# Sign product of a graph layer with two rows of x in one F32R matmul, interleaved with the first two row blocks of the aggregation

## The chip, the cores and the metric

The kernel runs on one NeuronCore of one Trainium2 chip. The metric is the device time of one execution in microseconds (us). The execution that the profiler recorded spans 2025.5 us. In what follows TensorE is called PE (its weight loads PEld), VectorE DVE, ScalarE ACT, GpSimd POOL and SyncE SP, as in the profile. SBUF is the on-chip memory that all engines read, PSUM the memory that TensorE adds its products into; the kernel uses it as eight banks of 128 x 512 fp32 numbers.

## What is computed

Two graph layers on x (4096 x 512) with an adjacency matrix adj (4096 x 4096), all fp32. The change is in layer 0 alone:

```python
bw = sign(weight)                 # 512 x 512, entries -1, 0, 1
ba = maximum(sign(x), 0.0)        # 4096 x 512, entries 0, 1
xw = ba @ bw.T                    # whole numbers from -512 to 512
x  = layernorm(x + relu(adj @ xw))
# layer 1: x @ edge_w, scores x' @ x'.T, two softmaxes, a product with adj,
# x @ weight and a second layernorm; it takes the larger part of the time
```

The product `ba @ bw.T` is called the sign product below, and `adj @ xw` the aggregation.

## The kernel before

P is 128, W 512 and D 512; NG = 8 groups of 512 rows, BG = 4 row blocks of 128 in each, NB = 32 row blocks in all, KD = 4 slices of 128 columns; HB = 16 and QC = 8. A tile pool hands out buffers: all tiles with one tag share `bufs` buffers, and a tile is written only when an earlier one of its tag has been read for the last time. The synchronisation between engines, and the order of instructions in the queue of each engine, are made by the framework from the data that the instructions touch; the order in the queues can differ from the written one.

The pools that matter: `stream` has 3 buffers (of 8 KB per partition), `rows` 4, `signs` (`sp`, tags `hi` and `lo`) 2 of each tag, `ps_mm` 6 banks of PSUM, `ps_tr` 2.

The sign product. For each group of 512 rows, the transposed x is loaded (`xt`), DVE compares it with zero into a bf16 tile `ba`, PE multiplies four row blocks by four slices, and ACT copies each finished bank into `xw`. In the first group, the weights are prepared slice by slice at the same time; twelve products of zeros run ahead while the first data are on their way.

```python
    warm = wp.tile([P, W], BF16, name="warm")
    nc.vector.memset(warm, 0.0)
    w0 = stream.tile([P, KD, D], F32, name="w0", tag="stream")
    bw = wp.tile([P, KD, D], BF16, name="bw")

    for g in range(NG):
        xt = stream.tile([P, KD, W], F32, name="xt", tag="stream")
        ba = sp.tile([P, KD, W], BF16, name="ba", tag="hi")
        pws = [ps_mm.tile([P, D], F32, name="pw", tag="mm") for j in range(BG)]
        if g == 0:
            neg = sp.tile([P, KD, D], BF16, name="neg", tag="lo")
            for k in range(KD):
                nc.sync.dma_start(w0[:, k, :], w0_t[ts(k, P), :])
                nc.scalar.dma_start(xt[:, k, :], x_t[ts(k, P), ts(g, W)])
            for _ in range(WARM):
                nc.tensor.matmul(pws[0], warm[:, :P], warm, start=True, stop=True)
            for k in range(KD):
                nc.vector.tensor_scalar(neg[:, k, :], w0[:, k, :], 0.0, None, ALU.is_lt)
                nc.vector.tensor_scalar(ba[:, k, :], xt[:, k, :], 0.0, None, ALU.is_gt)
                nc.vector.scalar_tensor_tensor(bw[:, k, :], w0[:, k, :], 0.0, neg[:, k, :], ALU.is_gt, ALU.subtract)
            order = [(k, j) for k in range(KD) for j in range(BG)]
        else:
            nc.sync.dma_start(xt, x_t[:, ts(g, W)].rearrange("(k p) n -> p k n", p=P))
            nc.vector.tensor_scalar(ba, xt, 0.0, None, ALU.is_gt)
            order = [(k, j) for j in range(BG) for k in range(KD)]
        for k, j in order:
            nc.tensor.matmul(pws[j], ba[:, k, ts(j, P)], bw[:, k, :], start=(k == 0), stop=(k == KD - 1))
            if k == KD - 1:
                nc.scalar.copy(xw[:, g * BG + j, :], pws[j])
```

The aggregation of one row block: adj comes in two halves of 16 x 128 x 128, each of which is worked in two quarters. F32R is a 32-bit format that the kernel takes to keep fewer bits than fp32, so ACT rounds a quarter to F32R (`hi`), DVE takes the rest (`lo`), and PE multiplies both with `xw` into one bank: 64 products for a row block. Then follow relu, the sum with x and the normalisation.

```python
    def aggregate(b):
        xb = rows.tile([P, D], F32, name="xb", tag="rows")
        nc.sync.dma_start(xb, x[ts(b, P), :])
        acc = ps_mm.tile([P, D], F32, name="acc", tag="mm")
        for half in range(2):
            at = stream.tile([P, HB, P], F32, name="at", tag="stream")
            nc.sync.dma_start(at, adj_t[b, :, ts(half, HB), :])

            for q in range(2):
                aq = at[:, ts(q, QC), :]
                hi = sp.tile([P, QC, P], F32R, name="hi", tag="hi")
                nc.scalar.copy(hi, aq)
                lo = sp.tile([P, QC, P], F32R, name="lo", tag="lo")
                nc.vector.tensor_sub(lo, aq, hi.bitcast(F32))
                for c in range(QC):
                    kb = half * HB + q * QC + c
                    nc.tensor.matmul(acc, hi[:, c, :], xw[:, kb, :], start=(kb == 0), stop=False)
                    nc.tensor.matmul(acc, lo[:, c, :], xw[:, kb, :], start=False, stop=(kb == NB - 1))
        nc.vector.scalar_tensor_tensor(xb, acc, 0.0, xb, ALU.max, ALU.add)
        layernorm([xb])
        scr = wp.tile([P, D], F32, name="scr")
        nc.vector.tensor_tensor_reduce(
            scr, xb, nw_b, 1.0, 0.0, ALU.mult, ALU.add, accum_out=node_s[:, b : b + 1]
        )
        nc.gpsimd.tensor_add(scr, xb, bias_b)
        nc.gpsimd.dma_start(x1_d[ts(b, P), :], scr)
        return xb
```

The loop over the row blocks takes them in the order 0, 16, 1, 17 and so on. After every second block POOL forms the sums for a later stage (`left`), and PE transposes each block's result with one block's delay:

```python
    before = None
    for n in range(NB):
        b = n // 2 + n % 2 * HB
        xb = aggregate(b)
        if n == 1:
            nc.sync.dma_start(we_s, edge_w.rearrange("(k p) o -> p k o", p=P))
        if n % 2:
            left(n // 2, before[1], xb)
        if before is not None:
            transpose_rows(*before)
        before = (b, xb)
    transpose_rows(*before)
# ... (layer 1 follows)
```

Of the kernel before, what the change touches and what calls it, by code (L numbers as in the profile page):

```python
# [11 lines left out]
F32 = mybir.dt.float32  # L12
BF16 = mybir.dt.bfloat16
F32R = mybir.dt.float32r
AF = mybir.ActivationFunctionType
ALU = mybir.AluOpType
# [3 lines left out]
EPS = 1e-5  # L20
NEG_BIG = -9000000000000000.0
HUGE = 3.4e38
WARM = 12


@with_exitstack
def kernel(
# [34 lines left out]
    make_identity(nc, ident)  # L62
    eps = const.tile([P, 1], F32, name="eps")
    nc.vector.memset(eps, EPS)
    node_s = const.tile([P, NB], F32, name="node_s")

    x1_d = dram.tile([N, D], F32, name="x1_d")
# [79 lines left out]
    with (  # L147
        tc.tile_pool(name="wide", bufs=1) as wide,
        tc.tile_pool(name="stream", bufs=3) as stream,
        tc.tile_pool(name="weights", bufs=1) as wp,  # L150
        tc.tile_pool(name="signs", bufs=2) as sp,
    ):
        x1T = wide.tile([P, KD, N], F32, name="x1T")

        warm = wp.tile([P, W], BF16, name="warm")
        nc.vector.memset(warm, 0.0)
        w0 = stream.tile([P, KD, D], F32, name="w0", tag="stream")
        bw = wp.tile([P, KD, D], BF16, name="bw")

        for g in range(NG):  # L160
            xt = stream.tile([P, KD, W], F32, name="xt", tag="stream")
            ba = sp.tile([P, KD, W], BF16, name="ba", tag="hi")
            pws = [ps_mm.tile([P, D], F32, name="pw", tag="mm") for j in range(BG)]
            if g == 0:
                neg = sp.tile([P, KD, D], BF16, name="neg", tag="lo")
                for k in range(KD):
                    nc.sync.dma_start(w0[:, k, :], w0_t[ts(k, P), :])
                    nc.scalar.dma_start(xt[:, k, :], x_t[ts(k, P), ts(g, W)])
                for _ in range(WARM):
                    nc.tensor.matmul(pws[0], warm[:, :P], warm, start=True, stop=True)  # L170
                for k in range(KD):
                    nc.vector.tensor_scalar(neg[:, k, :], w0[:, k, :], 0.0, None, ALU.is_lt)
                    nc.vector.tensor_scalar(ba[:, k, :], xt[:, k, :], 0.0, None, ALU.is_gt)
                    nc.vector.scalar_tensor_tensor(bw[:, k, :], w0[:, k, :], 0.0, neg[:, k, :], ALU.is_gt, ALU.subtract)
                order = [(k, j) for k in range(KD) for j in range(BG)]
            else:
                nc.sync.dma_start(xt, x_t[:, ts(g, W)].rearrange("(k p) n -> p k n", p=P))
                nc.vector.tensor_scalar(ba, xt, 0.0, None, ALU.is_gt)
                order = [(k, j) for j in range(BG) for k in range(KD)]
            for k, j in order:  # L180
                nc.tensor.matmul(pws[j], ba[:, k, ts(j, P)], bw[:, k, :], start=(k == 0), stop=(k == KD - 1))  # L181
                if k == KD - 1:
                    nc.scalar.copy(xw[:, g * BG + j, :], pws[j])

        nw_b = wp.tile([P, D], F32, name="nw_b")
        nc.sync.dma_start(nw_b, bass.AP(tensor=node_w.tensor, offset=node_w.offset, ap=[[0, P], [1, D]]))
        bias_b = wp.tile([P, D], F32, name="bias_b")
        nc.sync.dma_start(bias_b, bass.AP(tensor=bias.tensor, offset=bias.offset, ap=[[0, P], [1, D]]))
        we_s = wp.tile([P, KD, D], F32, name="we_s")


        def aggregate(b):
            xb = rows.tile([P, D], F32, name="xb", tag="rows")
            nc.sync.dma_start(xb, x[ts(b, P), :])
            acc = ps_mm.tile([P, D], F32, name="acc", tag="mm")
            for half in range(2):
                at = stream.tile([P, HB, P], F32, name="at", tag="stream")
                nc.sync.dma_start(at, adj_t[b, :, ts(half, HB), :])

# [20 lines that stand above are left out]
        def left(b, low, high):  # L220

            to = lop_d[b // BG][:, :, b % BG, :]
            l11, l21, l12, l22 = low[:, :HD], low[:, HD:], high[:, :HD], high[:, HD:]
            sums_l = wp.tile([P, 4, HD], F32, name="sums_l", bufs=2)
            s4, s1, s2, s3 = (sums_l[:, n, :] for n in range(4))
            nc.gpsimd.tensor_sub(s3, l11, l21)
            nc.gpsimd.tensor_add(s1, l22, l21)
            nc.gpsimd.tensor_sub(s2, s1, l11)
            nc.gpsimd.tensor_sub(s4, l12, s2)
            nc.gpsimd.dma_start(to[:, 0, :], l11)  # L230
            nc.gpsimd.dma_start(to[:, 1:4:2, :], high.rearrange("p (h f) -> p h f", h=2))
            nc.gpsimd.dma_start(to[:, 2, :], s4)
            nc.gpsimd.dma_start(to[:, 4:, :], sums_l[:, 1:, :])

        def transpose_rows(b, xb):
            pt = ps_tr.tile([P, KD, P], F32, name="pt", tag="tr")
            for k in range(KD):
                nc.tensor.transpose(pt[:, k, :], xb[:, ts(k, P)], ident)  # L238
            nc.scalar.copy(x1T[:, :, ts(b, P)], pt)
# [15 lines that stand above are left out]
        hT = big.tile([P, KD, N], F32, name="hT", tag="large")  # L255
        HK = KD // 2

        lops = stream.tile([P, 4, HK, HD], F32, name="lops", tag="stream")
        l11, l12 = we_s[:, :HK, :HD], we_s[:, HK:, :HD]
        l21, l22 = we_s[:, :HK, HD:], we_s[:, HK:, HD:]  # L260
        s4, s1, s2, s3 = (lops[:, n] for n in range(4))
        nc.gpsimd.tensor_add(s1, l21, l22)
        nc.gpsimd.tensor_sub(s2, s1, l11)
        nc.gpsimd.tensor_sub(s3, l11, l21)
        nc.gpsimd.tensor_sub(s4, l12, s2)
        left_h = l11, l12, s4, l22, s1, s2, s3
        for g in range(HG):
            r11, r12 = (x1T[:, :HK, ts(c, W)] for c in (g, g + HG))
            r21, r22 = (x1T[:, HK:, ts(c, W)] for c in (g, g + HG))
            t1, t2 = (sp.tile([P, HK, W], F32, name="t12", tag="hi") for _ in range(2))  # L270
            t3, t4 = (sp.tile([P, HK, W], F32, name="t34", tag="lo") for _ in range(2))
            nc.vector.tensor_sub(t1, r12, r11)
            nc.gpsimd.tensor_sub(t3, r22, r12)
            nc.vector.tensor_sub(t2, r22, t1)
            nc.vector.tensor_sub(t4, r21, t2)
            right_h = r11, r21, r22, t4, t1, t2, t3
            seven(
                lambda m, q: [left_h[m][:, k, ts(q, P)] for k in range(HK)],
                lambda m: [right_h[m][:, k, :] for k in range(HK)],
                [[hT[:, q + f, ts(c, W)] for f in (0, HK) for c in (g, g + HG)] for q in range(2)],  # L280
                lambda *_: None,
            )
# [357 lines left out]
```

## Time and profile before

| what | value |
|---|---|
| time, median of 3 runs | 2028.5 us (2028.37 to 2031.58) |
| span of the profiled execution | 2025.5 us, 17,689 instructions |
| PE / DVE / ACT / POOL busy | 99% / 61% / 34% / 20% |
| granted PE clock | 0.998 of full speed |
| moved by DMA | 455.73 MB, mean 225 GB/s |
| sign product on PE | 128 matmuls, starts from 6.2 to 37.3 us |
| aggregation of row blocks 0 and 16 on PE | 128 matmuls, starts from 37.3 to 66.6 us |

How to read it: a group of instructions is shown as line of the kernel, engine, operation, what it writes and reads, shape and count; after the first bar the busy time in us and the mean duration of one in ns; after the second the time the engine stood idle just ahead of them and what released it. Matmuls overlap, so the duration of one is its latency, and the rate is read from the distance between starts in the timeline. The profile names an idle time after the event that ended it; idle time of an engine that is not the limit costs nothing.

### The profile page before, as it was taken

The numbers are of one execution on the slowest core, as the hardware profiler recorded it, in microseconds if no ns is written. First come the engines' busy times: TensorE is split into PE (matmuls) and PEld (weight loads), VectorE is DVE, ScalarE is ACT, GpSimd is POOL, SyncE is SP. The second block draws the span as 40 slices with busy tenths as digits, with TensorE's granted clock in tenths as the row PEclk, the third lists the DMA queues.
The fourth block names the chain that finished last, engine by engine and source line by source line (L and its number), as shares of the span: only waits on it lengthen the run. The fifth ranks groups of instructions, "written<-read, shape, count | busy, mean of one in ns | idle before, by whom it ended". The sixth has DMA issues, their size and how long they took to land.

```text
span 2025.5 us, 17689 instructions
## 1 busy us (share of the span) xinstructions
PE 2004.4 (99%) x6268; PEld 1108.3 (55%) x6268; DVE 1243.5 (61%) x1759; ACT 691.5 (34%) x1195; POOL 401.5 (20%) x485
## 2 busy tenths in 40 slices
PE   9999999999999999999999999999999999999997
PEld 4888888888544454545555444444444444444443
DVE  3555555556534554445545897786759775977634
ACT  4333333333113666666666521131221220222100
POOL 0243333334300000000001111140124111321101
PEclk9999999999999999999999999999999999999999
DMA  9566566565009786867767887765666765685421
GB/s 328 186 220 203 196 216 210 201 209 173 29 0 351 260 302 229 308 231 272 280 257 265 330 329 258 250 248 198 249 237 251 260 246 201 227 283 201 172 70 62
DMA packets 118153, 455.73 MB, mean 225 GB/s; under 512 B 10288, under 2 KB 10288, under 8 KB 93488
## 3 DMA queue, kind: packets, MB, share of 16 engines
q0 software_dynamic: 48128, 241.20, 31.6%
q1 hardware_dynamic: 69360, 212.36, 31.6%
q8 instruction: 49, 0.80, 0.2%
q10 hardware_dynamic: 576, 1.05, 0.1%
q14 instruction: 40, 0.33, 0.0%
HBM read 355.99 MB, written 98.57 MB: 224 GB/s over the span
## 4 chain that ended last, share of the span: by engine, by line
PE 96%; DMA 3%; DVE 1%; ACT 0%; issue 0%; SPq 0%; ACTq 0%; POOLq 0%; POOL 0%; DVEq 0%
PE ps L479 38%; PE pe L356 21%; PE acc L209 11%; PE acc L208 11%; PE po L531 5%; PE seven L89 5%; PE pt L377 3%; DMA a<-in_adj_dram 2%; PE pw L181 1%; PE pt L238 1%; DMA xt<-in_x_t_dram 1%; DVE lo L205 0%; PE ptm L405 0%; DMA xb<-x_d 0%; ACT a L342 0%
## 5 line engine op out<-in xcount | busy, mean ns | idle before, releaser
L356 PE MATMUL pe<-hT 128*128 128x512 f32 (+3 forms) x1152 | 475.5, 557 | 0.0
L479 PE MATMUL ps<-q,lop 128*128 128x512 f32 x1024 | 446.9, 592 | 0.0
L208 PE MATMUL acc<-xw,hi 128*128 128x512 f32 x1024 | 401.6, 392 | 0.0
L209 PE MATMUL acc<-xw,lo 128*128 128x512 f32 x1024 | 399.4, 390 | 0.6 <-DVE lo L205 0.5
L479 PE MATMUL ps<-t,lop 128*128 128x512 f32 x768 | 332.9, 592 | 0.0
L479 PEld LDWEIGHTS ps<-q,lop 128*128 128x128 f32 x1024 | 193.9, 190 | 240.8 <-issue 237.0
L356 PEld LDWEIGHTS pe<-hT 128*128 128x128 f32 x1152 | 205.0, 191 | 184.0 <-issue 174.8
L434 ACT ACTIVATE q<-q 128x2048 f32<-128x2048 f32 x64 | 122.3, 1911 | 407.8 <-DVE q L431 394.2
L205 DVE TENSOR_TENSOR lo<-at,hi 128x1024 fp32r<-128x1024 f32 x128 | 168.7, 1318 | 147.1 <-ACT hi L203 147.1
L479 PEld LDWEIGHTS ps<-t,lop 128*128 128x128 f32 x768 | 145.9, 190 | 183.7 <-issue 180.3
L440 DVE SCALAR_TENSOR_TENSOR q<-ac,q 128x512 f32<-128x512 f32 x256 | 198.9, 830 | 53.6 <-ACT q L434 39.1
L203 ACT CAST hi<-at 128x1024 fp32r<-128x1024 f32 x128 | 134.6, 1052 | 272.6 <-PE acc L208 271.3
L209 PEld LDWEIGHTS acc<-xw,lo 128*128 128x128 f32 x1024 | 192.3, 188 | 41.0 <-DVE lo L205 1.7
L208 PEld LDWEIGHTS acc<-xw,hi 128*128 128x128 f32 x1024 | 192.3, 188 | 39.3
L338 DVE CUSTOM_DVE_ANT_0 a<-a,pe 128x512 f32<-128x512 f32 x112 | 76.7, 687 | 206.9 <-ACT s L363 206.9
L342 ACT ACTIVATE a<-a,nmax_c 128x512 f32<-128x512 f32 x256 | 183.5, 718 | 45.8 <-DVE nmax_c L338 45.5
L483 DVE TENSOR_TENSOR over<-over,ps 128x512 f32<-128x512 f32 x168 | 113.6, 681 | 107.8 <-PE ps L479 107.7
L431 DVE CUSTOM_DVE_ANT_1 q<-q,mrow 128x2048 f32<-128x2048 f32 x64 | 148.5, 2325 | 40.3 <-DMA q<-s_d 36.2
L363 ACT COPY s<-pe 128x512 f32<-128x512 f32 (+2 forms) x144 | 77.7, 543 | 138.4 <-PE pe L356 120.3
L531 PE MATMUL po<-over 128*128 128x512 f32 x256 | 115.9, 600 | 3.7 <-DVE xb L540 3.7
L425 POOL DMA_DIRECT2D ac<-in_adj_t_dram x64 | 48.8, 763 | 325.3 <-DVE q L440 253.4
L377 PEld LDWEIGHTS pt<-ident,s 128*128 128x128 f32 x496 | 62.1, 141 | 68.7 <-issue 57.7
(107 smaller groups left out, 1553.8 us busy)
## 6 DMA issues: line engine op xcount, KB each, us to landing
at<-in_adj_t_dram SPq DMA_DIRECT2D x64, 1024.0 KB, 5.1
ac<-in_adj_t_dram POOLq DMA_DIRECT2D x64, 1024.0 KB, 6.7
a<-in_adj_dram SPq DMA_DIRECT2D x64, 1024.0 KB, 7.5
q<-s_d POOLq DMA_DIRECT2D x64, 1024.0 KB, 7.8
lop<-lop_d SPq DMA_DIRECT2D x112, 512.0 KB, 4.1
s_d<-s POOLq DMA_DIRECT2D x36, 1024.0 KB, 4.8
s_d<-t POOLq DMA_DIRECT2D x28, 1024.0 KB, 6.2
xb<-in_x_dram SPq DMA_DIRECT2D x32, 256.0 KB, 3.1
```

Source lines behind the costliest of these rows:

```text
L203: nc.scalar.copy(hi, aq)
L205: nc.vector.tensor_sub(lo, aq, hi.bitcast(F32))
L208: nc.tensor.matmul(acc, hi[:, c, :], xw[:, kb, :], start=(kb == 0), stop=False)
L209: nc.tensor.matmul(acc, lo[:, c, :], xw[:, kb, :], start=False, stop=(kb == NB - 1))
L342: lambda: nc.scalar.activation(e, e, AF.Exp, bias=nmax_c[:, b, c : c + 1], scale=-1.0, accum_out=sum_c[:, b, c : c + 1])
L356: nc.tensor.matmul(pe[:, lo * P :], hT[:, k, ts(A * BG + i, P)], hT[:, k, (B * BG + lo) * P : (B + 1) * W], start=(k == 0), stop=(k == KD ...
L377: nc.tensor.transpose(pt[:, j, :], s[:, i, ts(j, P)], ident)
L431: nc.vector._custom_dve(TENSOR_ADD_SAT, out=q, in0=q, in1=mrow.unsqueeze(1).to_broadcast([P, BG, W]), s0=0.0, s1=-HUGE)
L434: nc.scalar.activation(q, q, AF.Exp)
L440: nc.vector.scalar_tensor_tensor(qc, a[:, :, c, :], 0.0, qc, ALU.max, ALU.mult)
L479: nc.tensor.matmul(ps, lop[:, c, ts(h, P)], rop[m][:, c, :], start=(c == 0), stop=(c == BG - 1))
L531: nc.tensor.matmul(po, (lower if k // 2 else upper)[:, k % 2, ts(i, P)], w1_s[:, k, :], start=(k == 0), stop=(k == KD - 1),)
```

## The change

It has two parts.

The first part computes two rows of x in one product. For rows a and b of the same group (b lies 256 rows further), `ba` now holds [a > 0] + 2048 [b > 0], in F32R. A product with the signs of the weights gives p = A + 2048 B in fp32, where A and B are the two wanted whole numbers, at most 512 in size, so both can be had from p exactly. Adding SHIFT = 1.5 x 2^34 rounds to a multiple of 2048, so u = SHIFT + 2048 B' (ACT); u - SHIFT - p is then minus the low part (DVE, out of PSUM), and a scaled copy of u gives minus the high part (ACT). The signs of the weights are negated (`bw` is now [w < 0] - [w > 0]), so the minus goes away. The number of sign products falls from 128 to 64, each with 128 x 128 weights and 512 columns as before, in F32R instead of bf16.

The second part moves the aggregation of row blocks 0 and 16 into the loop over the groups. As soon as a group's 512 rows of `xw` exist, the part of adj that meets them (4 x 128 x 128 for each of the two blocks) is loaded, split into hi and lo, and multiplied: 16 products for each group, written one group behind the sign product. Their two sums stay in the two `ps_tr` banks until the end; `aggregate` then finds them ready for these two blocks and does only the rest of its work. The purpose is to use the stretch of the sign product, in which the transfers of x are at work, for multiplications as well.

The buffers: the compare with the factor 2048 (`over0`) takes the tag `hi`, the incoming adj parts and the shifted sums `u` share the four `rows` buffers, `ba` shares a new tag `quarter` (2 buffers) with the later `sums_l`, and `bw` shares the buffer of `we_s`.

The diff, from the definitions on:

```diff
@@ -20,6 +20,8 @@
 EPS = 1e-5
 NEG_BIG = -9000000000000000.0
 HUGE = 3.4e38
+TWO = 2.0**11
+SHIFT = 1.5 * 2.0**34
 WARM = 12
 
 
@@ -62,6 +64,9 @@
     make_identity(nc, ident)
     eps = const.tile([P, 1], F32, name="eps")
     nc.vector.memset(eps, EPS)
+    shift = const.tile([P, 2], F32, name="shift")
+    nc.vector.memset(shift[:, 0:1], SHIFT)
+    nc.vector.memset(shift[:, 1:2], SHIFT / TWO)
     node_s = const.tile([P, NB], F32, name="node_s")
 
     x1_d = dram.tile([N, D], F32, name="x1_d")
@@ -155,32 +160,84 @@
         warm = wp.tile([P, W], BF16, name="warm")
         nc.vector.memset(warm, 0.0)
         w0 = stream.tile([P, KD, D], F32, name="w0", tag="stream")
-        bw = wp.tile([P, KD, D], BF16, name="bw")
-
-        for g in range(NG):
+
+
+        bw = wp.tile([P, KD, D], F32R, name="bw", tag="we_s")
+        assert D * 2 < TWO
+
+        def whole(g):
+
             xt = stream.tile([P, KD, W], F32, name="xt", tag="stream")
-            ba = sp.tile([P, KD, W], BF16, name="ba", tag="hi")
-            pws = [ps_mm.tile([P, D], F32, name="pw", tag="mm") for j in range(BG)]
+            ba = wp.tile([P, KD, W // 2], F32R, name="ba", tag="quarter", bufs=2)
+            pws = [ps_mm.tile([P, D], F32, name="pw", tag="mm") for j in range(BG // 2)]
+            order = [(k, j) for j in range(BG // 2) for k in range(KD)]
+
+            def signs(k, over):
+                a, b = xt[:, k, : W // 2], xt[:, k, W // 2 :]
+                nc.vector.tensor_scalar(over, b, 0.0, TWO, ALU.is_gt, ALU.mult)
+                nc.vector.scalar_tensor_tensor(ba[:, k, :], a, 0.0, over, ALU.is_gt, ALU.add)
+
             if g == 0:
-                neg = sp.tile([P, KD, D], BF16, name="neg", tag="lo")
+
+                pos = sp.tile([P, KD, D], BF16, name="pos", tag="lo")
+                over = sp.tile([P, KD, W // 2], F32, name="over0", tag="hi")
                 for k in range(KD):
                     nc.sync.dma_start(w0[:, k, :], w0_t[ts(k, P), :])
                     nc.scalar.dma_start(xt[:, k, :], x_t[ts(k, P), ts(g, W)])
                 for _ in range(WARM):
                     nc.tensor.matmul(pws[0], warm[:, :P], warm, start=True, stop=True)
                 for k in range(KD):
-                    nc.vector.tensor_scalar(neg[:, k, :], w0[:, k, :], 0.0, None, ALU.is_lt)
-                    nc.vector.tensor_scalar(ba[:, k, :], xt[:, k, :], 0.0, None, ALU.is_gt)
-                    nc.vector.scalar_tensor_tensor(bw[:, k, :], w0[:, k, :], 0.0, neg[:, k, :], ALU.is_gt, ALU.subtract)
-                order = [(k, j) for k in range(KD) for j in range(BG)]
+                    nc.vector.tensor_scalar(pos[:, k, :], w0[:, k, :], 0.0, None, ALU.is_gt)
+                    signs(k, over[:, k, :])
+                    nc.vector.scalar_tensor_tensor(bw[:, k, :], w0[:, k, :], 0.0, pos[:, k, :], ALU.is_lt, ALU.subtract)
+                order = [(k, j) for k in range(KD) for j in range(BG // 2)]
             else:
                 nc.sync.dma_start(xt, x_t[:, ts(g, W)].rearrange("(k p) n -> p k n", p=P))
-                nc.vector.tensor_scalar(ba, xt, 0.0, None, ALU.is_gt)
-                order = [(k, j) for j in range(BG) for k in range(KD)]
+                over = sp.tile([P, KD, W // 2], F32, name="over0", tag="hi")
+                nc.vector.tensor_scalar(over, xt[:, :, W // 2 :], 0.0, TWO, ALU.is_gt, ALU.mult)
+                nc.vector.scalar_tensor_tensor(ba, xt[:, :, : W // 2], 0.0, over, ALU.is_gt, ALU.add)
             for k, j in order:
                 nc.tensor.matmul(pws[j], ba[:, k, ts(j, P)], bw[:, k, :], start=(k == 0), stop=(k == KD - 1))
                 if k == KD - 1:
-                    nc.scalar.copy(xw[:, g * BG + j, :], pws[j])
+
+                    u = rows.tile([P, D], F32, name="u", tag="rows")
+                    nc.scalar.activation(u, pws[j], AF.Identity, bias=shift[:, 0:1])
+                    b = g * BG + j
+                    nc.vector.scalar_tensor_tensor(xw[:, b, :], u, SHIFT, pws[j], ALU.subtract, ALU.subtract)
+                    nc.scalar.activation(xw[:, b + BG // 2, :], u, AF.Identity, bias=shift[:, 1:2], scale=-1.0 / TWO)
+
+
+        early = [0, HB]
+        accs = []
+
+        def halves(g):
+
+            hi = sp.tile([P, QC, P], F32R, name="hi", tag="hi")
+            lo = sp.tile([P, QC, P], F32R, name="lo", tag="lo")
+            for n, b in enumerate(early):
+                a = rows.tile([P, BG, P], F32, name="a0", tag="rows")
+                nc.sync.dma_start(a, adj_t[b, :, ts(g, BG), :])
+                nc.scalar.copy(hi[:, ts(n, BG), :], a)
+                nc.vector.tensor_sub(lo[:, ts(n, BG), :], a, hi[:, ts(n, BG), :].bitcast(F32))
+            return hi, lo
+
+        def follow(g, hi, lo):
+            if g == 0:
+                accs.extend(ps_tr.tile([P, D], F32, name="acc0", tag="tr") for _ in early)
+            for n in range(2):
+                for c in range(BG):
+                    kb = g * BG + c
+                    nc.tensor.matmul(accs[n], hi[:, n * BG + c, :], xw[:, kb, :], start=(kb == 0), stop=False)
+                    nc.tensor.matmul(accs[n], lo[:, n * BG + c, :], xw[:, kb, :], start=False, stop=(kb == NB - 1))
+
+        whole(0)
+        parts = halves(0)
+        for g in range(NG):
+            if g + 1 < NG:
+                whole(g + 1)
+            follow(g, *parts)
+            if g + 1 < NG:
+                parts = halves(g + 1)
 
         nw_b = wp.tile([P, D], F32, name="nw_b")
         nc.sync.dma_start(nw_b, bass.AP(tensor=node_w.tensor, offset=node_w.offset, ap=[[0, P], [1, D]]))
@@ -192,8 +249,8 @@
         def aggregate(b):
             xb = rows.tile([P, D], F32, name="xb", tag="rows")
             nc.sync.dma_start(xb, x[ts(b, P), :])
-            acc = ps_mm.tile([P, D], F32, name="acc", tag="mm")
-            for half in range(2):
+            acc = accs[early.index(b)] if b in early else ps_mm.tile([P, D], F32, name="acc", tag="mm")
+            for half in range(0 if b in early else 2):
                 at = stream.tile([P, HB, P], F32, name="at", tag="stream")
                 nc.sync.dma_start(at, adj_t[b, :, ts(half, HB), :])
 
@@ -221,7 +278,7 @@
 
             to = lop_d[b // BG][:, :, b % BG, :]
             l11, l21, l12, l22 = low[:, :HD], low[:, HD:], high[:, :HD], high[:, HD:]
-            sums_l = wp.tile([P, 4, HD], F32, name="sums_l", bufs=2)
+            sums_l = wp.tile([P, 4, HD], F32, name="sums_l", tag="quarter", bufs=2)
             s4, s1, s2, s3 = (sums_l[:, n, :] for n in range(4))
             nc.gpsimd.tensor_sub(s3, l11, l21)
             nc.gpsimd.tensor_add(s1, l22, l21)

```

## The prediction

> **What bounds the kernel now.** I read the page first: busy time by engine, then the chain of work that ended last, then the groups of instructions.
>
> ```profile
> PE 2004.4 (99%) x6268; PEld 1108.3 (55%) x6268; DVE 1243.5 (61%) x1759; ACT 691.5 (34%) x1195; POOL 401.5 (20%) x485
> PE 96%; DMA 3%; DVE 1%; ACT 0%; issue 0%; SPq 0%; ACTq 0%; POOLq 0%; POOL 0%; DVEq 0%
> ```
>
> TensorE is busy for 99% of the span and 96% of the ending chain is TensorE. So a microsecond of matmul taken out comes off the end, unless a wait takes its place, and the change touches only the first 67 us. I therefore asked for busy time by stretch (columns: stretch and its length; busy us and instructions of PE, PEld, DVE, ACT, POOL; TensorE clock; DMA share; GB/s).
>
> ```profile
> 6.20:16.70 10.50, 7.73 (x33) 2.92 (x31) 6.32 (x11) 3.94 (x8) 0.00 (x0) 1.00 1.04 379
> 16.70:37.50 20.80, 20.73 (x97) 9.51 (x97) 6.97 (x7) 14.55 (x25) 0.00 (x0) 1.00 1.03 398
> 37.50:67.00 29.50, 29.44 (x131) 24.03 (x130) 13.38 (x16) 10.77 (x13) 4.02 (x4) 1.00 0.62 211
> ```
>
> The first two stretches are the sign product, the third is the first two row blocks of the aggregation. In the sign product the transfers are at their limit (about 390 GB/s, DMA share 1) and TensorE is full from 16.7 us on; before that it lost 2.8 us. In the aggregation TensorE is full, VectorE is at 45% (13.38 of 29.5), ScalarE at 37% and the transfers at 62%. The two stages have complementary slack: that is what the change goes for.
>
> The groups of instructions in the first 80 us give the prices:
>
> ```profile
> L208 PE MATMUL acc<-xw,hi 128*128 128x512 f32 x91 | 35.7, 393 | 0.0
> L181 PE MATMUL pw<-bw,ba 128*128 128x512 bf16 x128 | 28.6, 379 | 2.8 <-DVE ba L178 1.6 <-DVE bw L174 1.3
> L183 ACT CAST xw<-pw 128x512 fp32r<-128x512 f32 x32 | 18.3, 588 | 15.2 <-PE pw L181 15.1
> L205 DVE TENSOR_TENSOR lo<-at,hi 128x1024 fp32r<-128x1024 f32 x12 | 17.1, 1421 | 17.8 <-ACT hi L203 17.7
> L203 ACT CAST hi<-at 128x1024 fp32r<-128x1024 f32 x13 | 13.7, 1052 | 24.9 <-PE acc L208 23.7 <-PE acc L209 1.3
> L178 DVE TENSOR_SCALAR ba<-xt 128x2048 bf16<-128x2048 f32 x7 | 8.6, 1227 | 12.9 <-DMA xt<-in_x_t_dram 6.7 <-PE pw L181 6.2
> ```
>
> The mean of a matmul (379, 393 ns) is its latency. What counts is the distance of starts, which the timeline of TensorE shows:
>
> ```profile
> 16.77 20.89 PE L181 MATMUL pw<-bw,ba 128*128 128x512 bf16 x96 [0.24 <-DVE ba L178]
> ...
> 38.29 0.40 PE L208 MATMUL acc<-xw,hi 128*128 128x512 f32 x1
> ...
> 66.63 0.39 PE L209 MATMUL acc<-xw,lo 128*128 128x512 f32 x1
> ```
>
> Sign products (bf16): (20.89 - 0.38) / 95 = 216 ns apart. Aggregation (F32R): the 126 starts from 38.29 to 66.63 lie 227 ns apart (the trace lists 38.29, 38.52, 38.75 and so on; a transpose sits just behind the last). So F32R costs 5% more than bf16 per product of this shape, not a multiple.
>
> **What the Trainium skill says.** (1) "TensorE: Matmul & The Clock Gate", section "Wait — 56ns, not 53.3ns?", gives 215.7 ns between back-to-back warm matmuls of 512 columns; the trace has 216 for bf16. (2) The same page, "Weight-path perf modes — Fast Weight Load (FWL) and DoubleRow", says that the fast weight load is not for FP32. The trace agrees: a weight load takes 98 ns for the bf16 signs and 188 ns for the F32R aggregation. Both are shorter than the matmul beside which they lie, so the longer load should not show; 227 against 216 ns is all that I charge. (3) "VectorE: DVE Perf Modes", "Mode 2×_2P — use both read ports for one tensor", says that an fp32 operation with one tensor input can give two results a cycle from SBUF and one with two inputs cannot. The trace has 1227 ns for 2048 elements of the compare (one input) and 1.22 us for 1024 elements of the split's subtraction (two inputs). (4) "Perfetto Trace Analysis", "Identifying the Most-Contended Engine" warns that repeating gaps can mean that tiles cannot be allocated; this bears on the second rival.
>
> **The change, part by part.**
>
> *TensorE, signs.* Two rows share one product, so 16 matmuls per group become 8: 128 x 0.216 = 27.6 us become 64 x 0.227 = 14.5 us. That takes 13.1 us out, all of it on the path.
>
> *TensorE, aggregation.* The two row blocks keep their 128 matmuls, 128 x 0.227 = 29.0 us, in eight parts of 16 (3.63 us). Only their place changes.
>
> *VectorE, for each group of 512 rows.* Compare of 1024 elements with a factor: about 0.69 us (estimate from the 1227 ns row: fixed 0.16, then half of the rest). Compare-and-add of 1024 elements with two inputs: 1.23 (as the subtraction in L205 where nothing disturbs it). Two subtractions that take the low part out of PSUM: 2 x 0.69 (as the 692 ns of the 128x512 scalar_tensor_tensor in L210). Two lo halves of 512 elements: 2 x 0.69. Sum 4.7 us.
>
> *ScalarE, for each group.* Two shifted copies, two for the high part, two hi halves, six times some 0.58 us: 3.5 us.
>
> *Transfers.* 1.05 MB of x and 0.52 MB of adj for each group, 1.57 MB / 390 GB/s = 4.0 us.
>
> *TensorE, for each group.* 8 x 0.227 + 3.63 = 5.4 us. This is the largest of the four, so TensorE stays the bound if the engines run ahead of each other. VectorE at 4.7 is close behind.
>
> *The start.* The first group's VectorE work grows by about 0.23 us for each of four slices (half-width compare and add instead of one compare), so its last weights come at some 11.4 instead of 10.5 us and its eight products end near 12.1. The second group's x landed at 11.6 us before; 0.69 + 1.23 us of VectorE work bring its products to about 13.6. From there TensorE has 7 x 1.81 + 29.0 = 41.7 us of work. With no wait this ends at **55.3 us**, against 66.9 before: 11.6 us is the most that there can be. The two blocks' normalisation then comes at once, under the third block's matmuls, on a VectorE at 45%, and should cost nothing.
>
> *What I take off.* The shared VectorE queue is in order, and the new steps hand over from PE to ACT to DVE to ACT several times in each group. I allow half a microsecond in each of seven groups, 3.5 us. Gain 11.6 - 3.5 = 8.1 us: 2028.5 - 8.1 = **2020.4 us**, rounded to 2020.5.
>
> **The rivals.** (A) *The order of the queues.* If VectorE kept strictly to the written order, the compare for group g+2 would stand behind the lo halves of group g+1, which stand behind ScalarE's four PSUM steps of that group, which wait for its products. One turn would then be: products 1.8, landing 0.2, shift copy 0.58, high part 0.58, two hi copies 1.16, last lo 0.69, compare and add 1.92, hand-overs 0.5: 7.4 us instead of 5.4. Seven turns more than eat the gain: 7 x 2.0 = 14 us on top of 55.3, about 70 to 78 us for the stage, and 2032 to 2040 in all. Against it speaks that the trace before shows engines out of the written order: in block 0 a lo split runs between the two halves of the normalisation, and hi of the first block runs before the last three xw copies. I give this 8%.
>
> (B) *Buffers.* `rows` has four buffers, now shared by the shifted sums u and the incoming a; `hi` has two, shared by the compare's output and hi. In each group hi stays occupied from its copy to the end of its part, at least 0.58 x 2 + 0.69 + 3.63 = 5.5 us, so two buffers are just enough beside the compare's 1.9 us (7.4 us of 2 x 5.4). And an a can be fetched only when a u or an a came free; xb in the trace took 3.3 us to land at the median and up to 8.2. A late landing stalls hi, then lo, then TensorE. This would cost one or two us in some groups, up to 8 us in all, which leaves a time near the one before. I give it one in four in a strong form; the mild form is in the 3.5 us.
>
> (C) *The transfers.* 2.1 + 7.3 + 4.2 MB = 13.6 MB at 390 GB/s from about 1.7 us on are through at 36.6 us, long before the last group is needed at some 48 us. So bandwidth as such is not the bound. The early groups, though, are fed at 4.0 us each from 11.6 us on and want 5.4, so only the start can be short, by a microsecond or two.
>
> **Range and chances.** The best is 2028.5 - 11.6 = 2017; one more for the scatter between runs gives 2016 as the low end. A VectorE that is held in a few turns, or buffers in a strong form, leave 2025 to 2029; 2029 is the high end. Rival A alone lies outside. Two per cent are 40 us, more than the whole stage can win, and more than even rival A loses, so "within 2%" gets 0.985, faster 0.005, slower 0.01.
>
> **What would show it.** In the profile after: 64 sign matmuls and 128 of the two blocks, with starts 227 ns apart; TensorE done with both blocks at 57 to 61 us; VectorE's busy share in that stretch at 70% or more. Rival A would show as TensorE idle before the sign product, released by the compare-and-add on VectorE, about 2 us in each group; rival B as hi or a waiting for TensorE's last read or for a transfer. If the gaps sit between 6 and 16 us, my start was wrong; if the stretch from 67 us on has changed in length, something beyond the two blocks moved. Wrong would be the F32R price if sign matmuls lie more than 240 ns apart.

## The result, and the profile after

The changed kernel takes **2045.71 us** (median of 4 runs, 2043.21 to 2048.88) against 2028.72 us for the kernel before, a ratio of 1.0081 [1.0064, 1.0099]: 17 us slower, where the prediction had 8 us faster and a range up to 2029.

The page after, first line of the busy times and the chain that ended last:

```profile
PE 2006.6 (98%) x6204; PEld 1113.8 (54%) x6204; DVE 1256.9 (61%) x1796; ACT 696.6 (34%) x1203; POOL 403.1 (20%) x485
PE 94%; DMA 3%; DVE 1%; issue 0%; ACT 0%; SPq 0%; POOLq 0%; POOL 0%; ACTq 0%; DVEq 0%
```

TensorE lost its 64 matmuls (6268 to 6204), yet its busy time is no smaller and its share of the chain fell by two points. The last transpose of the aggregation starts at 542.7 us in the profiled run, against 523.0 before: 19.7 of the 21.6 us by which the two profiled spans differ are there (the profiled run is the slowest of the four), so nearly everything lies ahead of it. Busy time by stretch of the changed kernel (columns as in the prediction):

```profile
6.20:16.70 10.50, 3.83 (x9) 1.44 (x8) 6.62 (x16) 2.48 (x4) 0.00 (x0) 0.69 1.01 336
16.70:37.50 20.80, 13.55 (x48) 9.85 (x48) 8.97 (x12) 8.27 (x13) 0.00 (x0) 0.83 0.65 218
37.50:67.00 29.50, 23.34 (x77) 16.98 (x78) 15.79 (x21) 12.45 (x20) 0.00 (x0) 0.85 0.47 161
67.00:96.50 29.50, 26.61 (x104) 20.21 (x104) 16.45 (x25) 14.37 (x20) 7.43 (x8) 0.92 0.69 232
```

After 16.7 us nothing is full any more. Up to 67 us TensorE issues 125 matmuls where the kernel before issued 228; VectorE is busy for about half the time; the transfers are down from 398 and 211 to 218 and 161 GB/s; the granted clock is 0.83 and 0.85. Every engine and the transfers have slack at once, so the time goes into waits. The groups of the first 100 us name what TensorE waits for:

```profile
L230 PE MATMUL acc<-xw,hi 128*128 128x512 f32 x64 | 29.2, 457 | 19.1 <-ACT hi L220 19.1
L200 PE MATMUL pw<-bw,ba 128*128 128x512 f32 x64 | 19.6, 446 | 2.2 <-DVE ba L178 2.2
L220 ACT CAST hi<-a 128x512 fp32r<-128x512 f32 x16 | 9.6, 617 | 14.0 <-DMA a<-in_adj_t_dram 12.6 <-DVE over L197 1.3
L206 DVE SCALAR_TENSOR_TENSOR xw<-u,pw 128x512 fp32r<-128x512 f32 x16 | 10.9, 688 | 21.9 <-ACT u L204 21.9
```

L230 is the early aggregation, L200 the sign product. The idle time stands before the aggregation, 19.1 us, released by `hi`; and `hi` in turn waited 12.6 us for the part of adj (`a`) to land. The sign products hardly wait, and only in the first group. The start is one such wait; TensorE's timeline:

```profile
10.98 1.22 PE L200 MATMUL pw<-bw,ba 128*128 128x512 f32 x2 [0.74 <-DVE ba L178]
20.26 0.79 PE L230 MATMUL acc<-xw,hi 128*128 128x512 f32 x1 [8.05 <-ACT hi L220]
```

Then it repeats, group after group. I call a turn the time from one compare-and-add (`ba`, L198) to the next, a landing the time from the issue of a load to its arrival, and a split the making of `hi` and `lo` from a part of adj. The chain of waits within 46 to 66 us (start, us, what; first the shares by line):

```profile
by line: DMA a<-in_adj_t_dram 56.6%; DVE ba L198 18.4%; issue 12.7%; ACT hi L220 6.3%; PE acc L230 2.3%; SPq L195 1.9%; SPq L255 1.6%; PE acc L231 1.1%; DVE lo L221 1.1%; DVE over L197 0.2%; SPq L219 0.2%; ACTq L220 0.2%
...
47.70 1.23 DVE ba L198
...
48.95 0.38 SPq L195
...
49.42 5.62 DMA a<-in_adj_t_dram
...
55.12 0.63 ACT hi L220
...
55.77 0.04 DVE lo L221
55.81 0.57 issue
56.38 1.23 DVE ba L198
```

One turn is closed: compare-and-add `ba` 1.25 us to the next piece; then SP issues the load of the next x (L195), 0.47; behind it the two parts of adj, 5.70 until the first has landed; `hi` 0.65; the first `lo` 0.61; then the next `ba`. From 47.70 to 56.38 that is 8.68 us; over the whole stage `ba` starts 8.74 us apart (20.85 to 73.28 in six turns). TensorE, with its 24 matmuls (5.4 us), is not in this turn. The 3.4% of PE in the shares stand at the beginning of the stretch: in the turn before, the longest of the six (9.34 us), the compare waited for TensorE, whose clock was low. The queue of SP shows the order of issues:

```profile
48.95 0.38 SPq L195 DMA_DIRECT2D xt<-in_x_t_dram  x1
49.42 0.93 SPq L219 DMA_DIRECT2D a<-in_adj_t_dram  x2
```

The x load waits for a `stream` buffer, which `ba` frees by its last read; the adj parts stand behind it. Both blocks' products end at about 87.1 us (the last start and 0.23), where the kernel before was done at 66.9. TensorE's second group of sign products and its last product of the two blocks:

```profile
22.43 2.63 PE L200 MATMUL pw<-bw,ba 128*128 128x512 f32 x8
...
86.89 0.40 PE L231 MATMUL acc<-xw,lo 128*128 128x512 f32 x1
```

### The profile page after: what moved, and what is told of

The parts are those of the page before. It is cut to its first block, busy times and chain, and to the rows that moved or that the text cites. A ratio compares the mean times of both kernels' runs of the same rounds, so it can differ in the third digit from the quotient of the medians.

```text
span 2047.1 us, 17667 instructions
## 1 busy us (share of the span) xinstructions
PE 2006.6 (98%) x6204; PEld 1113.8 (54%) x6204; DVE 1256.9 (61%) x1796; ACT 696.6 (34%) x1203; POOL 403.1 (20%) x485
## 4 chain that ended last, share of the span: by engine, by line
PE 94%; DMA 3%; DVE 1%; issue 0%; ACT 0%; SPq 0%; POOLq 0%; POOL 0%; ACTq 0%; DVEq 0%
PE ps L536 38%; PE pe L413 21%; PE acc L266 11%; PE acc L265 11%; PE po L588 5%; PE seven L94 5%; PE pt L434 3%; DMA a<-in_adj_t_dram 2%; DMA a<-in_adj_dram 1%; PE pt L295 1%; PE acc L230 0%; PE acc L231 0%; DVE ba L198 0%; PE pw L200 0%; ACT hi L220 0%
## 5 line engine op out<-in xcount | busy, mean ns | idle before, releaser
L265 PE MATMUL acc<-xw,hi 128*128 128x512 f32 x960 | 376.7, 392 | 0.0
L266 PE MATMUL acc<-xw,lo 128*128 128x512 f32 x960 | 374.4, 390 | 0.2 <-DVE lo L262 0.2
L262 DVE TENSOR_TENSOR lo<-at,hi 128x1024 fp32r<-128x1024 f32 x120 | 157.2, 1310 | 127.4 <-ACT hi L260 127.4
L260 ACT CAST hi<-at 128x1024 fp32r<-128x1024 f32 x120 | 126.3, 1052 | 254.4 <-PE acc L265 253.9
L266 PEld LDWEIGHTS acc<-xw,lo 128*128 128x128 f32 x960 | 180.5, 188 | 38.0 <-DVE lo L262 1.2
L265 PEld LDWEIGHTS acc<-xw,hi 128*128 128x128 f32 x960 | 180.4, 188 | 36.8
```

## The experiments

The kernel before ran again beside each set of runs, with medians of 2027.4 to 2028.3 us. Each ratio is to the runs beside it; differences in us are between medians.

**The theory**, called Q in the expectations, from the chain above: the parts of adj come too late, and the delay is closed to a loop. Two things can do that, and I began with the first as the main one: the order in SP's queue, where adj stands behind an x load that waits for its buffer; and the common tag `rows`, of whose four buffers each group takes two for the sums `u` and two for adj, so that a part of the next group gets its place only when a split (`lo`) of the last one has been done. **The rivals:** (C) the clock, which is low after idle time, is the cause and not a consequence; or (H) VectorE and the hand-overs of the first part are the limit, and a mended load brings nothing.

### Parts of adj issued by POOL

```diff
-                nc.sync.dma_start(a, adj_t[b, :, ts(g, BG), :])
+                nc.gpsimd.dma_start(a, adj_t[b, :, ts(g, BG), :])
```

> The changed kernel with one word different: the parts of adj are issued from POOL's queue instead of SP's. Buffers as before. Theory Q (the loop goes through SP's queue: an adj part is issued behind the next x load, which waits for the compare-and-add, which stands on DVE behind the previous adj part): the loop of 8.6 us a group is cut; what is left is the wait for a rows buffer, about 6 us a group, both blocks done at 62 to 68 us instead of 87, total 2022 to 2030 us. Theory H (the loop goes through the hand-overs PE, ACT, DVE of the two-row products): nothing changes, 2041 to 2049. Theory C (the lower PE clock is the cost in itself): no change either unless the gaps go.

2037.96 us, ratio 1.0052 [1.0035, 1.0068]: 7.7 us better than the change, and far from the expectation. The turn fell to 7.4 us (`ba`, mean of six) but the loop stayed, as the chain of waits within 40 to 62 us shows (its shares add up to more than 100% because the first load in it began at 36.99 us):

```profile
by line: DMA a<-in_adj_t_dram 89.3%; issue 14.3%; DVE lo L221 9.4%; ACT u L204 6.2%; DVE over L197 3.1%; ACT hi L220 3.0%; DVE ba L198 1.0%; DVE xw L206 0.3%; ACT xw L207 0.1%; DVEq L221 0.1%
...
56.77 0.63 ACT hi L220
...
57.43 0.70 DVE lo L221
58.13 0.28 issue
58.41 6.47 DMA a<-in_adj_t_dram
```

and what POOL waited for up to 90 us (us in total, times, longest):

```profile
POOL a L219 <- DVE lo L221: 51.7, 12, 15.5
```

Here SP's queue is out of it, and still a part of adj is fetched 0.28 us after a split has freed its buffer: lo, load, hi, lo. So the queue's order, with which I had begun, is one part of the turn and no more; the buffers alone make a turn longer than TensorE's 5.4 us.

### Parts of adj land in memory of their own, all at once

The parts go, from POOL's queue, to places in the still empty tile `x1T`, a separate one for each of the sixteen.

```diff
-                a = rows.tile([P, BG, P], F32, name="a0", tag="rows")
-                nc.sync.dma_start(a, adj_t[b, :, ts(g, BG), :])
+                c0 = ((g // 4) * HB + (1 + g % 4 // 2) * BG) * P
+                a = x1T[:, 2 * n + g % 2, c0 : c0 + W].rearrange("p (c i) -> p c i", i=P)
+                nc.gpsimd.dma_start(a, adj_t[b, :, ts(g, BG), :])
```

> As the run with POOL's queue, and the parts of adj land in a stretch of x1T that is not yet in use, so that no part waits for a buffer. Theory Q: nothing of the loop is left, TensorE runs at its 5.4 us a group, both blocks done at 56 to 61 us, total 2018 to 2024 us. Theory H: still 7 us or more a group, total above 2032. If buffers alone were the cost, this and the run before differ by the whole loss.

2029.72 us, 1.0006 [0.9999, 1.0013]: 16 us better than the change, yet short of the expectation. Stretches, then TensorE's restart:

```profile
16.70:37.50 20.80, 16.54 (x64) 12.99 (x65) 13.30 (x19) 9.95 (x17) 0.67 (x2) 0.82 0.90 326
37.50:67.00 29.50, 29.00 (x124) 22.39 (x123) 22.25 (x31) 19.33 (x30) 0.00 (x0) 1.00 0.65 222
```

```profile
20.96 0.80 PE L231 MATMUL acc<-xw,hi 128*128 128x512 f32 x1 [5.91 <-DVE xw L206]
```

From 21 us on TensorE is full and a turn takes 6.1 us: the loop is gone. What stays lost is the start. With nothing to wait for, all 4 MB of adj are asked for from 1.3 us on and compete with the first slices of x and of the weights; the 1 MB loads of x issued by SP in the first 22 us landed 14.9 us after their issue (median; 6.8 in the kernel before).

### Each part of the change alone

Signs only: the first part with `early = []` and a plain loop `for g in range(NG): whole(g)`.

> The changed kernel with the first part of the change alone: two rows in one product, the aggregation of all 32 blocks after it as in the kernel before. Theory Q: no adj part, no loop; the sign product is then bound by the x loads (9.4 MB at 390 GB/s and the last group's work), TensorE starts the aggregation at 31 to 34 us instead of 37.3, total 2022 to 2026 us. Theory H: the hand-overs cost more than the products save, total at or above 2030.

2029.25 us, 1.0008 [1.0002, 1.0015]: no gain, below what I expected. Interleaving only: the bf16 signs of the kernel before, with the second part.

> The changed kernel with the second part alone: bf16 signs, one row in each product as before, and the two row blocks multiplied group by group beside it, adj parts on SP's queue. TensorE has the same 56.6 us of matmuls as before in this stage. The queue order of SP is another here: the adj part of a group stands ahead of the next x load. Theory Q: no loop of 8 us, both blocks done at 63 to 69 us, total 2024 to 2032 us. If interleaving as such costs (a rival: transfers and copies disturb each other), 2036 or more.

2027.76 us, 1.0001 [0.9993, 1.001], as expected. The middle stretch, signs only first, interleaving only second:

```profile
16.70:37.50 20.80, 14.15 (x48) 10.15 (x47) 18.46 (x24) 14.38 (x22) 0.00 (x0) 0.80 0.95 333
```

```profile
16.70:37.50 20.80, 20.80 (x95) 12.58 (x94) 8.83 (x11) 11.48 (x21) 0.00 (x0) 1.00 0.90 310
```

Fewer products alone leave TensorE idle for a third of the stretch, since the aggregation can't begin; interleaving alone keeps it full but takes no work away. Neither does anything by itself. And with bf16 signs there is no `u`: the same loads of adj then have all four buffers (and stand ahead of the x loads in SP's queue), and no loop arises: both blocks are done at 65.8 us.

### The sums get buffers of their own

```diff
-                    u = rows.tile([P, D], F32, name="u", tag="rows")
+                    u = rows.tile([P, D], F32, name="u", tag="u", bufs=2)
```

> The changed kernel with one line different: the shifted sums u have two buffers of their own, so that the four rows buffers serve the adj parts alone in this stage. An adj part need not wait for a u any more, and in SP's queue it then stands ahead of the next x load. Theory Q in its wider form (the loop is buffers and queue order together: adj part behind x load, x load behind compare-and-add, compare-and-add behind the split of the adj part): the loop is gone with this line alone, 5.5 to 6 us a group, both blocks done at 60 to 64 us, total 2021 to 2027 us. If SP's order is the whole cause and buffers play no part: 2036 or more, as the run with POOL's queue.

**2022.77 us**, 0.9975 [0.9966, 0.9985]: 23 us better than the change by one line, and faster than the kernel before. Stretches, waits from 12 to 60 us, and two issues of SP:

```profile
6.20:16.70 10.50, 7.38 (x18) 4.22 (x18) 9.38 (x21) 4.57 (x8) 0.00 (x0) 0.67 1.03 381
16.70:37.50 20.80, 20.34 (x87) 15.72 (x86) 15.09 (x21) 13.38 (x22) 0.00 (x0) 1.00 0.89 300
37.50:67.00 29.50, 28.25 (x123) 21.87 (x123) 23.16 (x34) 17.94 (x27) 3.12 (x3) 1.00 0.85 295
```

```profile
ACT hi L220 <- DVE ba L198: 11.5, 7, 1.9
...
PE acc L230 <- DVE xw L206: 1.8, 4, 1.1
```

```profile
24.20 0.93 SPq L219 DMA_DIRECT2D a<-in_adj_t_dram  x2
25.18 0.43 SPq L195 DMA_DIRECT2D xt<-in_x_t_dram  x1
```

The 19.1 us of TensorE behind `hi` are gone. What waits now is ScalarE, for the buffer of tag `hi` that the compare's output holds until `ba` has read it. TensorE starts again at 13.41 instead of 20.26 us, `ba` follows every 6.07 us, and both blocks are done at 59.2 instead of 87.1 us (again the last start and 0.23):

```profile
13.41 0.79 PE L230 MATMUL acc<-xw,hi 128*128 128x512 f32 x1 [1.07 <-DVE xw L206]
...
58.95 0.39 PE L231 MATMUL acc<-xw,lo 128*128 128x512 f32 x1
```

The two issues of SP show a side effect: with the buffers apart, the framework also put the parts of adj ahead of the x load. So this line removes both halves of the loop, and it can't divide them; the POOL run gives a hint, 7.7 us with the queue's order gone and the buffers still shared, the other 15 of the 23 us with the buffers apart too. How far the two add up was not tried.

Two more runs give adj places of its own in `x1T`, three for each of the two blocks (`g % 3`), so that the load runs ahead but not all at once; one from SP's queue, one from ACT's.

> The changed kernel, but the adj parts land in three places each within the unused x1T, reused every third group, still from SP's queue. In difference to the run in which all parts come at once, only two groups run ahead of the x loads at the start, so that the first x loads are not held up by 4 MB of adj. Wider theory Q: start of the second group at 14 to 16 us instead of 24, then 5.8 us a group: both blocks done at 59 to 62 us, total 2020 to 2025 us. If the slow start of that run was not the transfers, it ends where that run did, 2029.

> As the run before it, with the adj parts issued from ACT's queue, behind the first x slices; the second x load is then not behind any adj part on its queue. ACT pays the issues, some 0.4 us each, beside 4.1 us of work in a group of 5.8. Wider theory Q: 2019 to 2026 us; if ACT becomes the bound by it, 2027 or more.

2021.72 us, 0.9972 [0.9962, 0.9982] from SP, and 2025.0 us, 0.9985 [0.9978, 0.9991] from ACT. A second way of taking the buffers apart thus comes to the same time, and it says something on the two halves: from SP's queue each later pair of parts still follows an x load (x issued at 22.14, adj at 23.56 us, and likewise in the next two turns), yet from 12 us on `hi` never waits for a part, and both blocks are done at 58.5 us. With places enough to fetch ahead, that order does no harm. From ACT it is 3.3 us worse, and both blocks are done at 62.7 us: there a part of adj was issued at 0.73 us, ahead of the first four slices of x, whose issues then lasted until 5.18 us (2.57 in the run with `u` in its own buffers). Whether that is all of it was not tried.

### Is the clock the cause?

Ten idle products follow each group's aggregation in the changed kernel; nothing reads them.

```diff
             follow(g, *parts)
+            if g + 1 < NG:
+                keep = ps_mm.tile([P, D], F32, name="keep", tag="mm")
+                for _ in range(10):
+                    nc.tensor.matmul(keep, bw[:, 0, :P], xw[:, g * BG + BG - 1, :], start=True, stop=True)
```

> The changed kernel with ten idle products of 227 ns in each group, put where TensorE stands idle, so that its clock stays up. They write a bank that nobody reads. Theory C (the lower granted clock after each gap, 0.69 to 0.92 in these stretches, is a large part of the loss): 6 us or more are won, 2033 to 2040. Theory Q (the loop does not pass through TensorE at all): the period of the compare-and-add stays 8.6 to 8.8 us, total 2041 to 2048.

2044.95 us, 1.0092 [1.0076, 1.0107]. The stretch with the clock at 1.00:

```profile
37.50:67.00 29.50, 28.68 (x119) 21.70 (x118) 15.89 (x21) 12.84 (x20) 0.00 (x0) 1.00 0.49 164
```

The clock is full and the turn still 8.5 us, against 8.7 without the idle products, and the time is the same. The rival falls: the low clock is a consequence of the waits, and costs some 0.2 us a turn. But in the first group of the mended kernels it does cost something: there the stretch 6.2 to 16.7 us has 0.67. Idle products between the first group's sign products fill those gaps, put on both mended kernels:

```diff
                 nc.tensor.matmul(pws[j], ba[:, k, ts(j, P)], bw[:, k, :], start=(k == 0), stop=(k == KD - 1))
+                if g == 0 and j == BG // 2 - 1:
+                    for _ in range(3 if k < KD - 1 else 7):
+                        nc.tensor.matmul(keep, bw[:, k, :P], bw[:, k, :], start=True, stop=True)
```

> The version with buffers of their own for u, and in the first group 3 + 3 + 3 + 7 idle products between the sign products, into a bank that nobody reads, so that TensorE's clock is not lowered while the first slices arrive (0.67 from 6.2 to 16.7 us in the version without). If the slow matmuls that follow the start are on the path: some 18 matmuls get 0.2 us shorter each, 2 to 4 us less than without, 2018 to 2021 us. If the start is bound by the first loads and VectorE, no gain: 2022 to 2024.

> The same idle products in the version with three places in x1T. Its clock in that stretch was 0.84, so there is less to win: 0 to 2 us, 2019.5 to 2022 us.

**2019.81 us**, 0.9958 [0.9946, 0.9971], with `u` in its own buffers, and **2019.79 us**, 0.9957 [0.9943, 0.9971], with adj in `x1T`. These are the fastest of all, 8.3 us below the kernel before. The first of the two:

```profile
6.20:16.70 10.50, 10.17 (x40) 7.30 (x41) 9.59 (x20) 4.87 (x8) 0.00 (x0) 1.00 1.04 382
```

The clock is 1.00 instead of 0.67 and both blocks end at 57.3 us instead of 59.2. The 2 to 3 us between the mended kernels and these are a difference across two sets of runs, and the intervals of the ratios touch; the stretch and the end of the blocks show the direction, not the exact size.

### What limits the first part alone

Two runs, both on the signs-only kernel, tried whether VectorE is what keeps it at the old time. In one, POOL does the compare of the later groups (`nc.gpsimd.tensor_scalar` in place of `nc.vector.tensor_scalar`).

> The version with the first part of the change alone, where the compare with the factor runs on POOL instead of VectorE from the second group on. If VectorE was what bound that version (18.5 us busy of the 20.8 from 16.7 to 37.5 us), each group gets 0.6 us shorter and POOL with some 3 us a group stays below it: the aggregation starts at 33 to 36 instead of 38.6 us, total 2024 to 2027. If the transfers or the hand-overs bound it, no change, 2028 to 2030; if POOL is slower than that, 2030 or more.

2038.73 us, 1.0045 [1.0031, 1.0059]. The compare, in the groups of the first 80 us:

```profile
L197 POOL TENSOR_SCALAR over<-xt 128x1024 f32<-128x1024 f32 x7 | 29.6, 4232 | 13.5 <-DMA xt<-in_x_t_dram 13.1
```

4.23 us on POOL against 0.69 on VectorE: POOL became the limit, and the run says nothing of VectorE. In the other, the later groups' compare is left out: the first group's result, kept in `x1T`, is used for all, so the second rows of the later groups are not those of the reference.

> The version with the first part of the change alone, with one thing left out: from the second group on the compare with the factor (0.69 us of VectorE a group) is not done; the first group's is added in its place, so the high rows of the later groups are not those of the reference. Transfers, products, ScalarE's work and the output's shape are the same. If VectorE bound the version with the first part alone (18.5 us busy of 20.8), seven groups get some 0.6 us shorter: the aggregation starts at 34 to 36 us instead of 38.6, total 2024 to 2027 us. If transfers or hand-overs bound it, 2028 or more as before.

2030.93 us, 1.0013 [1.0004, 1.0022]. Taking 0.69 us a group off VectorE gains nothing, so the compare's share of VectorE does not limit the signs alone. In its chain between 16.7 and 41 us stand the sign products (34.5%), `ba` (20.3%) and the shifted copy (19.8%); the 29.0% of loads of x are one load that began at 10.65 us, for the most part ahead of the stretch. These are the hand-overs from engine to engine. Which link would have to be shortened stays open.

## Why the prediction was wrong

**What held.** The prices of the parts. Once nothing waits, eight sign products take 2.00 us in the mended kernel's timeline, (2.00 - 0.39) / 7 = 0.23 us apart: the F32R price. VectorE's steps measured 0.69 (compare), 1.22 (compare-and-add), 0.69 (low part) and 0.69 us (lo half), as estimated. ScalarE was a little dearer: 0.68 and 0.72 us for the two shifted copies, 0.62 for a hi half, together 2 x 2.02 = 4.0 us a group instead of 3.5; still under TensorE's 5.4.

**What failed: rival B, by its size.** The prediction saw that "an a can be fetched only when a u or an a came free" and that a late landing stalls hi, then lo, then TensorE; and it gave the sign for it, hi waiting for a transfer. The wait showed exactly there. But it was put down as one or two us in some groups, at most 8 in all, with its mild form inside the half microsecond of each group; and no rival had an adj part standing behind an x load in SP's queue. The missing step was to follow one buffer round: with two sums and two parts in each group, four buffers hold one group, so the next load begins only after the last split. The turn is then at least a landing and a split (`hi`, then `lo`), 5.7 + 0.65 + 0.61 = 7.0 us, with the issue of the x load and the compare-and-add 8.7, against 5.4 that TensorE needs. A wait that closes a loop is paid in every turn and can't be averaged with the turns in which it doesn't come. The last sentence of the skill's part of the prediction had pointed there: the Trainium skill, "Perfetto Trace Analysis", "Optimization Strategy", says that the same gap, repeated on the engine that should be full, can mean that there is not enough memory to allocate the next tile. The trace agrees with it: gaps before L230 in seven of the eight groups, and gone with two more buffers.

**The sum, term by term.** The prediction's best end for both blocks was 55.3 us; they ended at 87.1, 31.8 later. The second group's sign products began at 22.43 us instead of 13.6: 8.8 us. From there to the end it took 23.0 us more than TensorE's work, 3.3 in each of seven turns where 0.5 was allowed. In the start it was the queue's order alone: the first parts of adj were issued at 11.04 us, behind the load of the third group's x, and TensorE stood for 8.05 us; from POOL's queue, with the same buffers, they were issued from 1.48 us on, and TensorE stood for 2.65 us.

**Rival A** named a turn of 7.4 us through the queues, released by the compare-and-add. A loop of that kind came, but through a load and a buffer: the compare-and-add is in it because it frees the x buffer ahead of adj in SP's queue. TensorE's idle time was released by `hi`, so by the prediction's own sign it was B. **Rival C**, bandwidth, was rightly set aside for the stage as a whole (161 to 218 GB/s in it); the run that fetched everything at once shows that the start is where it counts.

**With the fault mended the working holds for the stage:** 55.3 + 3.5 = 58.8 us was predicted for the end of both blocks, and the kernel with `u` in its own buffers has 59.2; its time, 2022.77, is 2.4 us above the 2020.4. Part of the agreement is luck: of the 3.9 us above 55.3, 1.9 go with the low clock of the first group (57.3 with the idle products there), which the prediction did not have. And of the 7.7 us by which the stage got shorter, only 4.8 show in the time (2027.56 for the kernel before beside it); where the rest goes was not tried.

## What to carry to other kernels

When a change puts a new tile under an old tag, count the buffers along one turn: from the last read of the old tile through the issue, the landing and the first use of the new one. If that is longer than the bound engine's work in a turn, it becomes the period, however idle everything looks (here 8.7 us against 5.4). Before giving up such a change, give the tile its own buffers, and look at which load stands behind which in the issuing queue.

## What was not expected of the hardware

The clock fell already with short gaps. In the changed kernel TensorE waited for `hi` seven times, 19.1 us in all: 8.1 at the start, then 0.6 to 2.5. The granted clock was 0.83 and 0.85 in the two stretches from 16.7 to 67 us. That is a mean of pieces at full and at half rate, as the starts after two nearly equal gaps show:

```profile
37.77 0.80 PE L230 MATMUL acc<-xw,hi 128*128 128x512 f32 x1 [2.52 <-ACT hi L220]
...
39.09 0.63 PE L230 MATMUL acc<-xw,hi 128*128 128x512 f32 x1
39.51 0.63 PE L231 MATMUL acc<-xw,lo 128*128 128x512 f32 x1
...
55.79 0.49 PE L230 MATMUL acc<-xw,hi 128*128 128x512 f32 x1 [2.45 <-ACT hi L220]
...
56.86 0.40 PE L230 MATMUL acc<-xw,hi 128*128 128x512 f32 x1
57.10 0.40 PE L231 MATMUL acc<-xw,lo 128*128 128x512 f32 x1
```

After 2.52 us without a matmul the starts lie 0.42 us apart, and the granted clock from 37.77 to 41 us is 0.50; after 2.45 us they lie 0.24 us apart, and the clock from 55.79 to 60 us is 1.00. So this trace gives no length of gap at which the clock falls. The Trainium skill, "TensorE: Matmul & The Clock Gate", "Part 1: The HAM clock gate (the "warmup" mystery)", says that the clock goes to half after an idle window of about 3.4 us; the half rate is in the trace, but here it came after shorter gaps too. Ten idle products a group brought the clock to 1.00 from 37.5 to 67 us without moving the end.
